# Dealing the work beside the selective scans by its products, with one pair's convolutions moved behind them and the first unit set up differently

## The chip, the cores and the metric

The kernel runs on one core of one Trainium2 chip. The metric is the device time of one execution in microseconds (us); before the change the median of three runs is 3226.97, from 3225.29 to 3227.04. A core has engines with queues of their own that work in order: PE (TensorE, matrix products; its weight loads are counted apart as PEld), DVE (VectorE), ACT (ScalarE), POOL (GpSimd) and SP, which issues DMAs. They wait for each other by semaphores.

## The reference

The program is a stack of layers on an input of 8 images of 128 channels and 16 x 16 points: an adder convolution, a "mamba" fusion layer, an attention with a mixture of experts, a performer and a spectral layer. All the diff's effect is in the second, cut here to what matters:

```python
xn = layer_norm(x); u, z = split(xn @ in_proj_w.T)          # 256 channels each
for s in ("f", "b", "s"):                                   # forward, backward, sliced order
    uc    = silu(causal_conv1d(u_s, conv_w, conv_b))        # 4 taps, per channel
    proj  = uc @ xw.T                                       # dt (8), B (16), C (16)
    delta = softplus(dt @ dw.T + db)
    for n in range(16):                                     # states
        h_n = scan over l:  h = exp(delta * A_n) * h + delta * uc * B_n
    y_s   = sum_n h_n * C_n + uc * D
out   = ((y_f + y_b + y_s) * silu(z)) @ out_proj_w.T
attn  = softmax(y_f^T y_b);  out_a = y_s attn               # per image, over channels
out_a = conv3x3(out_a, fuse1)
x     = x + conv3x3(concat(out_a, out), fuse2)
```

## The kernel before

The second layer treats the images by pairs: four pairs of 512 columns, channels on the partitions, so that a full matrix product has 512 columns. All is 32-bit; a product shows in the profile as two records. A pair has three units, one for each scan order (f, b, s): twelve units in all, in the list `units`. A unit runs 16 rounds, one for each state n.

A round (in `_scans`) is: POOL multiplies `du` with the broadcast row B (`dbu`, L695; tile `db` has three buffers); ACT copies the row C into PSUM (`pcs`, L697); DVE runs two scans of 512 columns, one for each half of the 256 channels (`st`, L702), each of which takes a decay tile `da` (three PSUM banks in turn, refilled by an exponential on ACT, L658, `decays`); DVE multiplies by C (`hc`, L712, three buffers); PE adds `hc` to `acc` by two products with the identity. Before round 0 of a unit PE sets `acc` up with two products, and after round 15 ACT copies it out as `y` (L726 to L730).

Beside each round two generators advance, one step each: `more`, which prepares the next unit (`prepare`), and `other`, which does what belongs to the pair (`beside`). A step is what lies between two `yield`s.

- `prepare`: for s first z and its Silu. Then for each half the depthwise convolution as products with diagonal matrices (`pconv`; four for f and b, seven instructions for s), with its bias added on ACT (`pre`, L603); Silu as three ACT passes and a product (`silu`, L560 to L563), on POOL but in the very first unit on DVE; the projection `pp`, whose result is copied (`proj`, L611) and stored to DRAM rows by SP (L614); for each half the product `pd` and the softplus (L629 to L639, the last two on POOL); and `du` (L641). At round 14 what is left of it runs at once, and SP issues the first loads of the next unit's B and C rows (`chunk`, L650).
- `beside(p)`: the layer norm and the projection u of the next pair (`norm(p + 1)`), and then the finish of the pair before, `F.pair(p - 1)`: `attention` for each of its two images, `gated` (three POOL passes, L835 to L839, and the product `pm`) and `convolutions` (two 3x3 convolutions of 18 products each, tile `conv`, one step for each two products; the second ends with the addition to X on DVE, L869). In pair 0 it is `F.load()`, two DMAs of the convolution weights. What is left of it after a pair's third unit runs at once.

Thus the convolutions of pairs 0, 1 and 2 lie beside the scans of pairs 1, 2 and 3, and pair 3's finish runs behind all scans, in `mamba_layer`, with a PSUM pool of its own (`l1fps`, four banks), with its two images in step and most of its elementwise work on DVE (`F.alone`).

Before the first unit there is nothing to hide behind: `norm(0)` and the first `prepare` run one after the other (the set-up). `norm(0)` multiplies X by a centring matrix (identity less 1/128), which POOL makes at the start of `_scans` (L504).

Instructions are not issued in the order of the program text: a planner takes them engine by engine, by what is ready in its own model of the machine, and by the place in the text where several are. So the steps give priorities, not a fixed order. The performer layer behind raises the first 16 steps of its first stream (pairs 0 and 1) to the place marked by `E.mark`, the start of pair 3's finish.

Memory is given out in pools. A pool opened over memory that older pools have left waits either for all users of the older pools (the default), or, with `reuse_waits="tile"`, each tile for the older tiles under it. The performer's and spectral pools already have the latter. In the kernel before, `l1fps` lies over the three `da` banks and the bank of tag `s` in the scans' PSUM pools; `ln_rstd` and its neighbours in `l1one` lie over the adder layer's input x.

Of the kernel before, what the change touches and what calls it, by code (L numbers as in the profile page):

```python
# [207 lines left out]
class Env:  # L208


    def __init__(self, ctx, tc, dram, cols):
        self.tc, self.nc, self.dram = tc, tc.nc, dram
        self.cols = cols
        nc = self.nc
        pool = ctx.enter_context(tc.tile_pool(name="shared", bufs=1))
        self.pool = pool
        self.cst = pool.tile([P, dram["cst"].shape[1]], F32, tag="cst", name="cst")
        self.vecs = pool.tile([P, dram["vecs"].shape[1]], F32, tag="vecs", name="vecs")
        self.rows = pool.tile([P, dram["rows"].shape[1]], F32, tag="rows", name="rows")
        self.mean = pool.tile([P, P], F32, tag="mean", name="mean")  # L220
        self.ones = pool.tile([P, P], F32, tag="ones", name="ones")
        self.eps = pool.tile([P, 1], F32, tag="eps", name="eps")
        self.sg = pool.tile([P, NK], F32, tag="sg", name="sg")
        nc.gpsimd.memset(self.mean, 1.0 / P)
        nc.gpsimd.memset(self.ones, 1.0)
        nc.gpsimd.memset(self.eps, 1e-5)
        self.X = pool.tile([P, NT], F32, tag="X", name="X")

        self.early = ExitStack()
        early = self.early.enter_context(tc.tile_pool(name="early", bufs=1))  # L230
        self.w = {
            k: (pool if k in ("tok", "enc", "dec") else early).tile(
                list(dram[k].shape), F32, tag="w_" + k, name="w_" + k
            )
            for k in ("in_proj", "xproj", "dtproj", "out_proj", "tok", "enc", "dec")
        }

        self.diag = early.tile([P, 3, 2, 5, P], F32, tag="diag", name="diag")
# [84 lines left out]
def adder_layer(E):  # L323
# [8 lines left out]
    with ExitStack() as ctx:  # L332
# [54 lines left out]
        for kw in range(3):  # L387
            t = p.tile([P, B, 18 * 16], F32, tag=f"sh{kw}", name=f"sh{kw}")
            nc.gpsimd.tensor_copy(t.rearrange("p b (h w) -> p b h w", w=16), pad[:, :, :, kw : kw + 16])
            shifted.append(t)  # L390
        diagonals(E)
# [66 lines left out]
NPAIRS = B // UB  # L458
CN = 2


def mamba_layer(E):


    tc = E.tc
    with ExitStack() as ctx:
        F = _Fuse(E, ctx)
        with ExitStack() as inner:
            _scans(E, inner, F)
        F.psum = ctx.enter_context(tc.tile_pool(name="l1fps", bufs=4, space=PSUM))  # L470
        F.alone = True
        E.mark = tc.cur_priority
        for _ in F.pair(NPAIRS - 1):
            pass
# [11 lines left out]
def _scans(E, ctx, F):  # L486
# [7 lines left out]
    one = ctx.enter_context(tc.tile_pool(name="l1one", bufs=1))  # L494
    two = ctx.enter_context(tc.tile_pool(name="l1two", bufs=2))
    scratch = ctx.enter_context(tc.tile_pool(name="l1dram", bufs=2, space=bass.MemoryType.DRAM))
    pda = ctx.enter_context(tc.tile_pool(name="l1pda", bufs=1, space=PSUM))
    ps = ctx.enter_context(tc.tile_pool(name="l1ps", bufs=1, space=PSUM))
# [4 lines left out]
    center = one.tile([P, P], F32, tag="center", name="center1")  # L503
    nc.gpsimd.tensor_sub(center, E.c("ident"), E.mean)  # L504
    three = ctx.enter_context(tc.tile_pool(name="l1three", bufs=3))
    xn, us = {}, {}

    def norm(p):

        first = p == 0  # L510
        src = E.X[:, blk(p)]
        pxc = ps.tile([P, UT], F32, tag="s" if first else "f", name="xc1")
        E.mm(pxc, center, src)
        xc = one.tile([P, UT], F32, tag="ln_xc", name="ln_xc")
        if first:
            nc.vector.tensor_copy(xc, pxc)
        else:
            nc.scalar.copy(xc, pxc)
        rstd = one.tile([P, UT], F32, tag="ln_rstd", name="ln_rstd")
        nc.scalar.activation(rstd, pxc, AF.Square)  # L520
        yield
        var = ps.tile([P, UT], F32, tag="f", name="var1")
        E.mm(var, E.mean, rstd)
        nc.scalar.activation(rstd, var, AF.Ln, bias=E.eps)

        nc.scalar.activation(var, rstd, AF.Exp, scale=-0.5)
        yield
        t = xn[p] = two.tile([P, UT], F32, tag="xn", name="xn1")
        nc.vector.tensor_mul(t, xc, var)
        nc.scalar.activation(t, t, AF.Identity, scale=E.v("ln_w"), bias=E.v("ln_b"))  # L530
        yield
        us[p] = two.tile([P, 2, UT], F32, tag="u", name="u1")
        for h in range(2):
            pu = ps.tile([P, UT], F32, tag="s" if first and h else "f", name="pu")
            E.mm(pu, E.w["in_proj"][:, h * P : (h + 1) * P], t)
            dst = us[p][:, h, :]
            if first and h:
                nc.vector.tensor_copy(dst, pu)
            else:
                nc.scalar.copy(dst, pu)  # L540
            yield
# [15 lines left out]
    def silu(dst, src, gen):  # L557

        t = one.tile([P, 2, UT], F32, tag="sig", name="sig")
        nc.scalar.activation(t, src, AF.Exp, scale=-1.0)  # L560
        nc.scalar.activation(t, t, AF.Ln, bias=E.ones[:, 0:1])
        nc.scalar.activation(t, t, AF.Exp, scale=-1.0)
        gen.tensor_mul(dst, src, t)  # L563
        return t

    def prepare(k, s, p, got, first=False):
        u = us[p].rearrange("p h (b l) -> p h b l", l=L)
        if s == "s":
# [6 lines left out]
            yield  # L575
            silu(z, z, nc.gpsimd)
            yield
        uc = two.tile([P, 2, UT], F32, tag="uc", name="uc")
        pre = one.tile([P, 2, UT], F32, tag="pre", name="pre")
        for h in range(2):  # L580
# [15 lines left out]
            for j, (m, out, src) in enumerate(taps):  # L596
                E.mm(out, E.diag[:, k, h, 3 - m, :], src, start=j == 0, stop=j == len(taps) - 1)
            dst = pre[:, h, :].rearrange("p (b l) -> p b l", l=L)
# [5 lines left out]
            yield  # L604
        room = silu(uc, pre, nc.vector if first else nc.gpsimd)
        yield
# [9 lines left out]
        yield  # L616
# [6 lines left out]
        for h in range(2):  # L623
# [7 lines left out]
            yield  # L631
# [4 lines left out]
            yield  # L636
# [3 lines left out]
            yield  # L640
        gen.tensor_mul(du, delta, uc)  # L641
        got.update(delta=delta, du=du)
        yield
# [9 lines left out]
    turns = [0, 0]  # L653

# [6 lines left out]
    def beside(p):  # L661
# [4 lines left out]
        else:  # L666
            yield from F.pair(p - 1)
# [7 lines left out]
    for i, (k, s, p) in enumerate(units):  # L675
# [8 lines left out]
        for n in range(NST):  # L684
# [30 lines left out]
            next(more, None)  # L715
            next(other, None)
# [18 lines left out]
class _Fuse:  # L735


    def __init__(self, E, ctx):
        self.E = E
        nc, tc = E.nc, E.tc  # L740
        one = ctx.enter_context(tc.tile_pool(name="l1fone", bufs=1, side="right"))
        self.two = ctx.enter_context(tc.tile_pool(name="l1ftwo", bufs=2, side="right"))
        self.four = ctx.enter_context(tc.tile_pool(name="l1ffour", bufs=4, side="right"))
# [23 lines left out]
    def pair(self, p):  # L767
        images = [self.attention(self.y[p], b) for b in range(UB)]
        if self.alone:
            while images:  # L770
                images = [g for g in images if next(g, None)]
        else:
# [3 lines left out]
        yield from self.convolutions(p)  # L776

    def attention(self, y, b):
# [4 lines left out]
        for k in range(2):  # L783
# [7 lines left out]
            yield True  # L791
# [13 lines left out]
        yield True  # L805
# [6 lines left out]
        yield True  # L812
# [6 lines left out]
        yield True  # L819
# [7 lines left out]
        yield True  # L827

    def gated(self, p):
# [6 lines left out]
        yield True  # L836
        gen.tensor_add(g, g, y[:, 2])
        yield True
        gen.tensor_mul(g, g, self.z[p])  # L839
        yield True  # L840
# [7 lines left out]
        yield True  # L848

    def convolutions(self, p):  # L850
        E, nc = self.E, self.E.nc
        for j in range(2):
            out = self.bank([P, UT], "conv")
            for n in range(18):
# [3 lines left out]
                if n % 2:  # L858
                    yield True
# [10 lines left out]
            yield True  # L870
# [193 lines left out]
def performer_layer(E, W):  # L1064
# [3 lines left out]
    with ExitStack() as ctx:  # L1068
# [19 lines left out]
        S.center = one.tile([P, P], F32, tag="center", name="center")  # L1088
        nc.vector.tensor_sub(S.center, S.c("ident"), S.mean)
# [529 lines left out]
```

## Time and profile before

| what | us | from |
|---|---|---|
| median of three runs | 3226.97 | times |
| the profiled execution | 3226.58 | times |
| its span | 3224.5 | page |
| adder layer, to the last addition to X | 0 to 988.5 | timeline |
| set-up to the first scan | 988.65 to 1032.50 | timeline |
| scans, 192 rounds | 1032.50 to 1799.36 | timeline |
| pair 3's finish | 1799.4 to 1854.6 | timeline |
| the layers behind | 1854.6 to 3224.5 | timeline |

| engine | busy us over the span | share |
|---|---|---|
| PE | 2994.3 | 93% |
| DVE | 2395.7 | 74% |
| ACT | 2208.3 | 68% |
| POOL | 733.2 | 23% |

A line of the timeline or of a group names the line of the code, the engine, the instruction, the output and its inputs, the shape and how many records; in brackets is how long the engine had been idle before and what ended that. Nearly all matrix products have the line of one helper, L271, and so are told apart by tiles. Shares over the whole span say little about this change: PE's 93% is an average over an adder layer and a performer that keep it full, and the scans, where DVE has the most to do. What a change in the scans is worth must be read there.

### The profile page before, as it was taken

How to read it: one execution, taken by the hardware profiler on the slowest of the kernel's cores; microseconds unless marked ns; L12 is line 12 of the kernel's file. 1: busy time of each engine (PE TensorE's matmuls, PEld its weight loads, DVE VectorE, ACT ScalarE, POOL GpSimd, SP SyncE). 2: the span in 40 equal slices, each digit the busy share in tenths (PEclk: the TensorE clock that was granted, in tenths of full speed). 3: DMA queues.
4: the chain of work that ended last, by engine and by line, in shares of the span. 5: the costliest groups of instructions: out<-in, count | busy, mean ns of one | idle time of the engine just before them, and what ended most of it. 6: DMA issues, size and time to landing. Idle time of an engine off the chain costs nothing.

```text
span 3224.5 us, 42745 instructions
## 1 busy us (share of the span) xinstructions
PE 2994.3 (93%) x16814; PEld 1335.5 (41%) x16814; DVE 2395.7 (74%) x3288; ACT 2208.3 (68%) x2639; POOL 733.2 (23%) x420
## 2 busy tenths in 40 slices
PE   6999999999997888888988789999999999999999
PEld 2333332333332333333343345555555555555444
DVE  6999999999995999788897466665665566564531
ACT  6999999999995877677675243666657766667111
POOL 3000000000002888677786100100000010010110
PEclk9999999999998999999999999999999999999999
DMA  1000000000001544333343100000000000000200
GB/s 38 1 1 5 1 1 4 1 1 5 1 1 59 178 146 136 124 126 126 120 143 115 47 27 14 1 15 1 15 14 1 15 14 1 14 1 3 86 27 13
DMA packets 39197, 132.53 MB, mean 41 GB/s; under 512 B 7490, under 2 KB 10572, under 8 KB 36564
## 3 DMA queue, kind: packets, MB, share of 16 engines
q1 hardware_dynamic: 38564, 129.07, 11.9%
q8 instruction: 132, 2.16, 0.3%
q10 hardware_dynamic: 432, 0.73, 0.1%
q14 instruction: 69, 0.57, 0.1%
HBM read 126.91 MB, written 1.84 MB: 40 GB/s over the span
## 4 chain that ended last, share of the span: by engine, by line
PE 69%; DVE 14%; ACT 6%; issue 5%; POOL 4%; DMA 1%; DVEq 0%; POOLq 0%; ACTq 0%; SPq 0%
PE o L271 29%; PE p L271 8%; DVE hc L712 4%; DVE st L702 4%; PE g L271 3%; PE pc L271 3%; PE acc L271 2%; PE pq L271 2%; PE xc L271 2%; PE pa L271 2%; PE conv L271 2%; PE pn L271 2%; PE pb L271 2%; PE var L271 1%; PE po L271 1%
## 5 line engine op out<-in xcount | busy, mean ns | idle before, releaser
L271 PE MATMUL o<-d,sel 128*32 128x512 f32 x8800 | 946.5, 592 | 3.2 <-DVE d L437 3.2
L439 ACT ACTIVATE d<-sh,w 128x2048 f32<-128x2048 f32 x460 | 886.3, 1996 | 64.2 <-PE o L271 54.8
L437 DVE TENSOR_SCALAR d<-sh,w 128x2048 f32<-128x2048 f32 x640 | 787.0, 1287 | 48.9 <-PE o L271 41.0
L271 PEld LDWEIGHTS o<-d,sel 128*32 128x32 f32 x8800 | 298.2, 110 | 650.7 <-issue 540.9
L695 POOL TENSOR_TENSOR dbu<-du,bs 128x1024 f32<-128x1024 f32 x191 | 449.2, 2365 | 171.8 <-DVE st L702 75.1
L702 DVE TENSOR_TENSOR_SCAN st<-da,dbu 128x512 f32<-128x512 f32 x384 | 448.4, 1206 | 30.5 <-POOL dbu L695 17.9
L271 PE MATMUL acc<-hc,cst 128*128 128x512 f32 x768 | 369.2, 609 | 56.6 <-DVE hc L712 56.3
L658 ACT ACTIVATE da<-delta,neg_a 128x510 f32<-128x510 f32 x384 | 260.0, 688 | 118.2 <-DVE st L702 112.8
L712 DVE TENSOR_TENSOR hc<-st,pcs 128x1024 f32<-128x1024 f32 x192 | 229.9, 1197 | 48.1 <-PE acc L271 38.8
L1278 POOL TENSOR_TENSOR rk<-rk,ro 128x512 f32<-128x512 f32 x32 | 40.8, 1274 | 911.6 <-DVE ro L1277 911.6
L271 PEld LDWEIGHTS acc<-hc,cst 128*128 128x128 f32 x768 | 140.6, 192 | 249.4 <-issue 139.0
L748 POOL MEMSET pad<- 128x1296 f32 x2 | 2.3, 1177 | 952.3 <-PE o L271 952.3
L1551 ACT COPY ug<-p 128x512 f32<-128x512 f32 x64 | 37.5, 586 | 176.3 <-PE p L271 176.3
L697 ACT COPY pcs<-cs 128x512 f32<-128x512 f32 x192 | 113.5, 591 | 57.9 <-DVE hc L712 55.6
L271 PE MATMUL p<-u,lw 128*128 128x512 f32 x256 | 132.7, 637 | 16.5 <-ACT ek L1323 14.7
L271 PE MATMUL conv<-pad,f 128*128 128x512 f32 x288 | 135.7, 601 | 8.6 <-ACT pad L845 4.4
L431 DVE SCALAR_TENSOR_TENSOR d<-sh,w,d 128x2048 f32<-128x2048 f32 x52 | 122.3, 2351 | 1.9
L271 PE MATMUL p<-T,H 128*128 128x512 f32 x256 | 114.4, 596 | 5.7 <-DVE ug L1553 4.7
L1374 ACT ACTIVATE qp<-px,keps 88x512 f32<-88x512 f32 x128 | 84.2, 678 | 50.9 <-PE px L1373 50.5
L271 PE MATMUL p<-g,lw 128*128 128x512 f32 x256 | 114.6, 595 | 0.8 <-ACT g L1216 0.8
L271 PE MATMUL g<-ug,me 128*128 128x512 f32 (+1 forms) x320 | 112.0, 509 | 2.0 <-DVE me L1539 2.0
L1323 ACT ACTIVATE ek<-ek 128x352 f32<-128x352 f32 x128 | 60.1, 493 | 62.8 <-DVE ek L1320 62.7
(317 smaller groups left out, 4166.9 us busy)
## 6 DMA issues: line engine op xcount, KB each, us to landing
bs<-rows SPq DMA_DIRECT2D x96, 512.0 KB, 3.8
cs<-rows SPq DMA_DIRECT2D x96, 512.0 KB, 4.7
lw<-in_layers SPq DMA_DIRECT2D x8, 1076.0 KB, 4.9
m<-in_Mphi SPq DMA_DIRECT2D x8, 1024.0 KB, 4.9
f<-in_fuse SPq DMA_DIRECT2D x2, 1152.0 KB, 7.7
T<-in_T SPq DMA_DIRECT2D x1, 2064.0 KB, 8.0
x<-in_x SPq DMA_DIRECT2D x4, 256.0 KB, 6.3
total<-sums SPq DMA_DIRECT2D x16, 64.0 KB, 2.0
```

The lines of the kernel that those rows point to most:

```text
L271: self.nc.tensor.matmul(out, lhsT=lhsT, rhs=rhs, start=start, stop=stop)
L431: nc.vector.scalar_tensor_tensor(held, tap(k), w[:, k, f : f + 1], held, ALU.max, ALU.add)
L437: nc.vector.tensor_scalar(d, tap(k), wk, None, ALU.max)
L439: nc.scalar.activation(d, tap(k), AF.Abs, scale=-1.0, bias=wk)
L658: nc.scalar.activation(das[turns[0] % 3][:, :, 1:], d[:, :, 1:], AF.Exp, scale=a)
L695: gen.tensor_tensor(db, got["du"], bc(got["bs", c][:, j, :], 1, 2), ALU.mult)
L697: nc.scalar.copy(pcs, got["cs", c][:, j, :])
L702: nc.vector.tensor_tensor_scan(st[:, h, :], da.rearrange("p b l -> p (b l)"), db[:, h, :], 0.0, ALU.mult, ALU.add)
L712: nc.vector.tensor_tensor(hc, st, bc(pcs[:, :], 1, 2), ALU.mult)
L1278: nc.gpsimd.tensor_add(r, r, o)
L1323: nc.scalar.activation(e, e, AF.Exp, scale=0.5)
L1374: nc.scalar.activation(qp[:, :, c * P : (c + 1) * P], px, AF.Identity, bias=S.keps[0:PAIR, :])
```

## The change

- **Dealing.** Every step now yields a cost, about the number of 512-column products that it holds (0.1 for a step without any). A round gets a budget of `SHARE` = 2.25; what `more` costs is taken off (one step a round, as before), and `other` advances as long as some budget is left; an overdraft carries over to the next round.
- **Finer steps.** A half's depthwise convolution is cut into two steps, a 3x3 convolution yields after each product. The softplus has one step less a half: the subtraction and addition on POOL follow its exponentials without a yield between.
- **The third pair's convolutions.** `F.pair` is split into `before` (attention and gate) and `convolutions`. In pair 3 the scans only take `before(2)`; pair 2's convolutions run behind the scans, four steps of them after each step of pair 3's attention and gate, and then pair 3's.
- **The first unit.** Silu's three passes and its product are done for each half as soon as the half is there. The centring matrix is made in the adder layer, in the shared pool, and the performer uses the same one. `norm(0)` works on the centred values in PSUM, without a copy, and writes its reciprocal root to SBUF.
- **Pools.** All pools of the layer get `reuse_waits="tile"`. The Silu's work tile of z and of uc are taken apart by name (same tag).

```diff
@@ adder_layer
+        nc.gpsimd.tensor_sub(E.center, E.c("ident"), E.mean)
         diagonals(E)
@@ mamba_layer
-        F.psum = ctx.enter_context(tc.tile_pool(name="l1fps", bufs=4, space=PSUM))
+        F.psum = ctx.enter_context(tc.tile_pool(name="l1fps", bufs=4, space=PSUM, reuse_waits="tile"))
         F.alone = True
         E.mark = tc.cur_priority
-        for _ in F.pair(NPAIRS - 1):
-            pass
+        last = NPAIRS - 1
+        convs = F.convolutions(last - 1)
+        for _ in F.before(last):
+            for _ in range(4):
+                next(convs, None)
+        for p in (convs, F.convolutions(last)):
+            for _ in p:
+                pass
@@ _scans, norm
-        E.mm(pxc, center, src)
-        xc = one.tile([P, UT], F32, tag="ln_xc", name="ln_xc")
-        if first:
-            nc.vector.tensor_copy(xc, pxc)
-        else:
+        E.mm(pxc, E.center, src)
+        xc = pxc
+        if not first:
+            xc = one.tile([P, UT], F32, tag="ln_xc", name="ln_xc")
             nc.scalar.copy(xc, pxc)
...
-        nc.scalar.activation(var, rstd, AF.Exp, scale=-0.5)
+        r = rstd if first else var
+        nc.scalar.activation(r, rstd, AF.Exp, scale=-0.5)
@@ _scans, prepare
             for j, (m, out, src) in enumerate(taps):
                 E.mm(out, E.diag[:, k, h, 3 - m, :], src, start=j == 0, stop=j == len(taps) - 1)
+                if j + 1 == len(taps) // 2:
+                    yield 2
...
-            yield
-        room = silu(uc, pre, nc.vector if first else nc.gpsimd)
-        yield
+            if h == 0:
+                room = one.tile([P, 2, UT], F32, tag="sig", name="sig")
+            if first:
+                silu(uc[:, h, :], pre[:, h, :], room[:, h, :], nc.vector)
+            yield 2
+        if not first:
+            silu(uc, pre, room, nc.gpsimd)
+            yield 0.1
...
             nc.vector.scalar_tensor_tensor(e, one_e, -1.0, e, ALU.add, ALU.subtract)
-            yield
             nc.scalar.activation(r, one_e, AF.Ln)
             gen.tensor_sub(r, r, e)
             gen.tensor_add(d, d, r)
-            yield
+            yield 0.1
@@ _scans, beside and the rounds
-            yield from F.pair(p - 1)
+            yield from F.before(p - 1)
+            if p + 1 < NPAIRS:
+                yield from F.convolutions(p - 1)
...
-            next(more, None)
-            next(other, None)
+            budget = min(budget, 0) + SHARE - next(more, 0)
+            while budget > 0:
+                cost = next(other, None)
+                if cost is None:
+                    break
+                budget -= cost
@@ _Fuse.convolutions
-                if n % 2:
-                    yield True
+                yield 1
```

The costs given elsewhere: 1 for each step of `norm` but its scaling (0.1); 2 for z's products, 2 for a half of a depthwise half, 2 for `pp`, 1 for each `pd`; in attention 0.6 for each set of four transposes, 2 for the scores, 2 for the output, 0.1 for the scaling; in the gate 0.1 for each of the three passes and 2 for `pm`; 0.1 behind each 3x3 convolution.

## The prediction

> **What bounds the kernel now.** I read the table of stages first, then DVE's waits inside the scans, then PE's timeline where they are longest, then the two ends: the first unit's set-up and the stretch behind the scans. All times are of the profiled execution (3226.58 us, span 3224.5), 0.4 us below the median of the runs, 3226.97; my sum is made against 3226.6.
>
> By stages (columns: stretch, its length, busy us of PE, weight loads, DVE, ACT, POOL, granted clock, DMA share, GB/s). The first four are the four pairs of images in the scans, cut where the last `hc` of a pair's 48 rounds ends; the fifth is what stands behind them.
>
> ```profile
> 1037.10:1203.90 166.80, 133.50 (x292) 50.92 (x292) 163.89 (x150) 130.97 (x210) 141.66 (x67) 0.98 0.48 161
> 1203.90:1402.30 198.40, 170.91 (x414) 73.52 (x414) 172.17 (x158) 138.18 (x229) 152.11 (x71) 0.98 0.39 131
> 1402.30:1607.00 204.70, 179.33 (x432) 76.64 (x432) 172.69 (x159) 142.36 (x236) 150.67 (x71) 0.96 0.38 124
> 1607.00:1799.40 192.40, 163.56 (x398) 72.05 (x398) 170.01 (x156) 126.33 (x209) 135.81 (x71) 0.96 0.37 127
> 1799.40:1854.60 55.20, 48.55 (x138) 25.44 (x138) 11.68 (x25) 5.92 (x18) 0.11 (x1) 0.94 0.04 17
> ```
>
> Pair 0 has DVE busy for 163.9 of 166.8 us: it is bound by the scans, and its undisturbed rounds repeat every 3.36 us. Pairs 1 and 2 carry the finish of the pair before (attention, gate, two 3x3 convolutions) and last 198.4 and 204.7 with DVE busy only 172: 58.2 us are lost. Pair 3 loses 22.4. DVE's waits in pairs 1 and 2 (1204 to 1607; total us, times, longest):
>
> ```profile
> DVE hc L712 <- PE acc L271: 27.3, 8, 6.0
> DVE st L702 <- POOL dbu L695: 10.0, 4, 3.8
> DVE hc L712 <- ACT da L658: 4.5, 1, 4.5
> DVE st L702 <- ACT da L658: 4.2, 3, 2.4
> ```
>
> In pair 3 the first two are 11.5 and 6.5. `hc` has three buffers, so it waits for `acc` only when PE is three rounds of backlog behind. How that comes about, in pair 3's second unit:
>
> ```profile
> 1695.85 3.71 PE L271 MATMUL pconv<-u,diag 128*128 128x512 f32 x14 [1.46 <-ACT pre L603]
> ...
> 1699.39 1.88 PE L271 MATMUL conv<-pad,f 128*128 128x512 f32 x4
> ...
> 1703.10 1.22 DVE L712 TENSOR_TENSOR hc<-st,pcs 128x1024 f32<-128x1024 f32 x1 [4.94 <-PE acc L271]
> ```
>
> One round got a whole half of the depthwise convolution and convolution products on top of its own two; DVE stood for 4.94 us. Behind the scans PE is nearly full:
>
> ```profile
> 1796.93 1.98 PE L271 MATMUL acc<-hc,cst 128*128 128x512 f32 x4 [1.38 <-DVE hc L712]
> 1799.41 1.98 PE L271 MATMUL acc<-hc,cst 128*128 128x512 f32 x4 [0.50 <-DVE hc L712]
> 1802.56 1.97 PE L787 MATMUL pt<-cst,y 128*128 128x128 f32 x16 [1.16 <-ACT y L730]
> ...
> 1811.59 1.09 PE L816 MATMUL pt<-cst,at 128*128 128x128 f32 x4 [2.61 <-DVE at L809]
> 1813.81 0.45 PE L816 MATMUL pt<-cst,at 128*128 128x128 f32 x1 [1.13 <-DVE at L809]
> ...
> 1821.52 15.62 PE L271 MATMUL conv<-pad,f 128*128 128x512 f32 x36
> ```
>
> A 512-column product is two records; 36 records in 15.6 us make **0.86 us a product** back to back. That unit is used below.
>
> **Part 1, ahead of the scans.** Now `center` (POOL, 0.45) starts only when the last X addition is out, and the first product waits for it:
>
> ```profile
> 988.65 0.45 POOL L504 TENSOR_TENSOR center<-cst,mean 128x128 f32<-128x128 f32 x1 [3.24 <-DVE X L452]
> 989.16 2.07 PE L271 MATMUL xc<-X,center 128*128 128x512 f32 x2 [6.19 <-POOL center L504]
> ```
>
> With the matrix made early and tile-wise reuse, the product needs X's first block alone (985.68 + 0.71 = 986.4) and is done by 988.5. Its square on ACT, at 991.99 before, needs `ln_rstd`'s bytes, which lie in the old x that the last addition reads until 988.55: about 988.65, so 3.3 us earlier. That takes the product 2.1 (hidden behind the additions), the copy `ln_xc` 0.7 and center 0.5 off the path. POOL's subtraction moves into the first layer, where POOL is idle: nothing. If the wait is by block rather than by tile it is 5; if something else in the old bytes is late, 1. Silu by halves: behind the last `pre`, three ACT passes of 1024 columns (1.06 + 1.15 + 1.06) and one DVE product (1.23) become 512-column ones; rows of that size take 0.60, 0.69, 0.60 and 0.69: 4.5 against 2.6, 1.9 saved; the first half's pass lies under the second half's products (pre ends 1008.4 and 1011.8). Together **-5.2**, bounds -2.5 and -7.
>
> At one place here the clock matters. The four xproj records `pp` took 3.32 us after PE had idled 5.39; in the scans the same four take 1.91, and the granted clock was 0.82 from 1002 to 1032. [...] I take nothing for it.
>
> **Part 2, the dealing, pairs 1 and 2.** Work now comes by cost: each round gets 2.25 products beside its own two. A pair's cost by the new yields: preparing f and b 12.4 each, s 14.5; norm 4.1; attention and gate 14.1; convolutions 36.2: 93.7 in 48 rounds, so 41.6 rounds at 4.25 products, 3.66 us on PE (above DVE's 3.36), and 6.4 at 3.36: 152.3 + 21.5, plus six first products of `acc`, 5.2: **179** against DVE's busy 172. No round now gets more than 5 products. So the 27.3 us on `acc` go, and the pacing replaces them. What dealing does not touch: waits for POOL 10.0, for `da` 8.7, for `pcs` 4.0, 22.7 in all; a DVE wait in a PE-paced round lets PE catch up, so I count half, 11.4. PE's own waits for POOL's `uc` before `pp` (12.3 us in 8 places from 1204 to 1800) stay, with three convolution products between in place of two; about 4 in these pairs. 2 x 179 + 15.4 = 373 against 403.1: **-30**. Bounds: -48 (DVE busy 344.9 plus the POOL waits alone) and +10 (the old waits stay and the pacing is paid too). Pair 0 has 1.5 us of POOL wait and bursts to lose: **-2**, 0 to -3.
>
> What the moved steps issue: F.load's two DMAs on SP go from about round 5 to round 6 of the first unit; their first user is at 1298. The `rows` store on SP comes two rounds later (7 us); its loads are issued at round 14, more than 5 rounds behind. Delta's last step keeps its round (the tenth for f and b). In the gate three POOL passes of 2.36 now fall in one round, since each costs 0.1; POOL's lead is `db`'s three buffers, two rounds or 6.7 us, against 7.1: small, and inside the bounds.
>
> **Part 3, pair 3 without convolutions.** DVE busy 170.0, less the X addition 0.7, plus the waits for POOL and small ones (6.5 + 2.0), plus a quarter of the `acc` waits (those at attention in the first unit stay, 3): 181 against 192.4: **-12**; bounds -18 and -5.
>
> **Part 4, behind the scans.** 36 products come here: 36 x 0.86 = 31.0. They can fill PE's idle 0.50 + 1.16 + 2.61 + 1.13 = 5.4: **+25.8**. Upper bound +31. `l1fps` lies over the banks of the three `da` and of `s`; tile-wise, `s`'s bank is free all through the last unit and `da2`'s before the last round, where PE idles 1.38 a round. If the scheduler pulls attention and convolutions there, and the next layer's first half starts beneath the convolutions, it is +10. I take +25.8, since three banks come free only at the end. The 0.93 between the last two convolutions and the last X addition stay; the SBUF tiles and performer's work keep their sizes.
>
> Sum: -5.2 - 30 - 2 - 12 + 25.8 = -23.4, **3203 us**.
>
> **Rivals.** (A) Slower: PE has no slack left at 4.25 products a round, and its in-order queue still waits for POOL's `uc`, itself behind gate passes; each such wait is now paid in full. For: PE idled 12.3 us before `pp`, POOL is busy 152 of 198. Pairs 1 and 2 then keep their length (0), pair 3 gains 5, the ends -2.5 and +31: 3250. It decides as soon as pairs 1 and 2 together gain less than 6.6 (25.8 - 5.2 - 2 - 12). Against: PE in these pairs is busy 171 and 179 of about 200, so 50 us of slots exist. (B) The convolutions only change place: pair 3 gains 12, pairs 1 and 2 about 15, the tail costs 31, with -5.2 and -2 elsewhere: -3, 3223; within what can be told. For: 31 us of work into a stretch that is 88% PE. (C) Better than summed: pairs 1 and 2 near DVE's bound (-42), pair 3 -16, tail +18 because bank `s` and the performer's head start fill it: -47, 3179. For: the free bank and the 1.38 us gaps. (D) The change doesn't do what it says: the order on each engine is the planner's, by what is ready, so that the convolutions are pulled back among pair 3's last rounds; the tail is then +10 and the last unit 5 longer, 3192: inside the forecast's range.
>
> **How the numbers follow.** Forecast with D 0.51, C 0.22, B 0.10, A 0.17. The predicted time is the forecast's. 0.2% (6.5 us) is about what can be told from no change, and B alone lies within it. Faster 0.73, same 0.10, slower 0.17. Range: down to C, up past 3226 until little of A is inside: 3177 to 3232.
>
> **What would show it.** Right: DVE's waits for `acc` in pairs 1 and 2 under 10 us, rounds of 3.6 to 3.7 with few above 6, the pairs 183 to 190 long; pair 3 near 180; 72 more `conv` records behind the scans and that stretch some 80 us; the first scan 5 us earlier. Wrong: pairs still near 200 with waits now for POOL or `da`, or the stretch behind the scans over 90.

## The result, and the profile after

The changed kernel takes **3300.43 us** (median of four runs, 3297.98 to 3301.82), beside 3226.91 for the kernel before on the same chip (four runs, 3225.29 to 3227.04). The ratio is 1.0228, with a 95% interval from 1.0210 to 1.0246: slower, where 3203 and "faster" had been predicted, and above the range's end of 3232. The profiled execution's span is 3297.7 us against 3224.5, so 73.2 us have to be found.

The stages of the kernel after, cut in the same way as those of the kernel before (columns: stretch, its length, busy us of PE, weight loads, DVE, ACT, POOL, granted clock, DMA share, GB/s):

```profile
1032.40:1217.90 185.50, 141.43 (x297) 53.41 (x296) 163.73 (x151) 131.88 (x211) 141.82 (x67) 0.94 0.43 145
1217.90:1431.90 214.00, 180.13 (x414) 76.83 (x415) 173.03 (x158) 137.48 (x228) 150.11 (x71) 0.91 0.36 119
1431.90:1654.00 222.10, 185.01 (x432) 78.63 (x432) 174.46 (x159) 141.40 (x236) 150.66 (x71) 0.93 0.34 115
1654.00:1847.70 193.70, 142.06 (x326) 60.03 (x326) 167.42 (x154) 125.17 (x207) 137.90 (x71) 0.90 0.39 128
1847.70:1926.10 78.40, 77.30 (x212) 37.78 (x212) 12.55 (x25) 6.75 (x20) 0.11 (x1) 1.00 0.03 12
```

DVE has about the same work as before in every pair (163.7, 173.0, 174.5 and 167.4 us against 163.9, 172.2, 172.7 and 170.0), and each pair is longer, pair 0 too, which has no finish of another pair beside it. Pair 3 lost its 72 `conv` records (398 to 326) and is no shorter. The granted clock is lower in all four pairs: 0.94, 0.91, 0.93 and 0.90 against 0.98, 0.98, 0.96 and 0.96. Where the 73.2 us lie, the tail being the time from the last scan round to the last addition to X, and the forecast of -30 for pairs 1 and 2 halved between them (the terms are rounded, so the last digit of a row's sum may differ):

| us | to the first `hc` | pair 0 | pair 1 | pair 2 | pair 3 | tail | layers behind | sum |
|---|---|---|---|---|---|---|---|---|
| forecast | -5.2 | -2 | -15 | -15 | -12 | +25.8 | 0 | -23.4 |
| measured | -4.6 | +18.7 | +15.6 | +17.4 | +1.3 | +23.2 | +1.7 | +73.2 |

The two ends came as forecast. The 12 units' scans did not. DVE's waits inside all scans of the kernel before, and then of the kernel after (total us, times, longest):

```profile
DVE hc L712 <- PE acc L271: 38.8, 12, 6.0
DVE st L702 <- POOL dbu L695: 17.9, 7, 4.9
```

```profile
DVE hc L728 <- PE acc L272: 45.8, 18, 7.0
DVE st L718 <- POOL dbu L711: 45.2, 13, 8.7
DVE hc L728 <- ACT pcs L713: 16.7, 13, 2.8
```

The waits for `acc`, which the dealing was to remove from pairs 1 and 2, are still there (in these two pairs alone 39.7 us, for 27.3 before). The waits for `dbu` grew from 17.9 to 45.2 us. And PE itself, in the kernel before and in the kernel after, from the same view:

```profile
PE pp L271 <- POOL uc L563: 15.2, 11, 3.0
```

```profile
PE pp L272 <- POOL uc L571: 43.0, 11, 5.6
```

PE stands at `pp`, the projection of the next unit, for 43.0 us in 11 places; the prediction had priced that at about 4 in pairs 1 and 2.

**Where the `dbu` waits sit.** I measured each of the 192 rounds from the end of one `hc` to the end of the next. Of the eleven first rounds (round 0 of every unit but the first) I add up what is over 3.36 us: 2.8 us in the kernel before and **50.0 us** in the kernel after, where the longest last 13.9, 12.3 and 18.2 us. The start of the last unit in the kernel after, on POOL (timeline; columns: start, length, instruction, in brackets the idle time before it and what ended that):

```profile
1778.23 1.27 POOL L651 TENSOR_TENSOR sig<-sig,pre 128x512 f32<-128x512 f32 x1 [9.20 <-ACT sig L650]
...
1786.03 1.27 POOL L651 TENSOR_TENSOR sig<-sig,pre 128x512 f32<-128x512 f32 x1 [5.18 <-ACT sig L650]
...
1788.72 2.34 POOL L654 TENSOR_TENSOR du<-delta,uc 128x1024 f32<-128x1024 f32 x1
1791.14 9.25 POOL L711 TENSOR_TENSOR dbu<-du,bs 128x1024 f32<-128x1024 f32 x4
```

and what DVE's timeline has for it:

```profile
1784.49 0.69 DVE L649 SCALAR_TENSOR_TENSOR pre<-one_e,pre 128x512 f32<-128x512 f32 x1 [4.55 <-ACT one_e L648]
1793.51 3.52 DVE L718 TENSOR_TENSOR_SCAN st<-da,dbu 128x512 f32<-128x512 f32 x3 [8.33 <-POOL dbu L711]
```

The old unit's scans are over; the new unit's softplus is still going through PE, ACT and POOL; `du` is out at 1791.06 and the first scan follows `dbu`, after 8.33 us in which DVE had nothing. In the kernel before the same `du` was out at 1735.54 and DVE stood for 4.86 there, its longest wait for `dbu`. In the kernel after the preparation comes too late. The means over all 11 preparations, and in the last column the sum of the first rounds:

| kernel | `pp` starts after the unit's first scan | `pp` to the end of `du` | `du`'s end against the unit's last scan | first rounds over 3.36, sum |
|---|---|---|---|---|
| before | 32.7 | 27.2 | 2.2 early | 2.8 |
| after | 40.4 | 26.5 | 3.0 late | 50.0 |

`dbu` takes 2.36 us behind `du`, and a scan cannot start before it. So the kernel before had on the mean no margin left to give, and the change took 5.2 us.

### The profile page after: what moved, and what is told of

Its sections match the earlier page's. It is cut to its first block, busy times and chain, and to the rows that moved or that the text cites. A ratio compares the mean times of both kernels' runs of the same rounds, so it can differ in the third digit from the quotient of the medians.

```text
span 3297.7 us, 42745 instructions
## 1 busy us (share of the span) xinstructions
PE 3025.5 (92%) x16814; PEld 1344.4 (41%) x16814; DVE 2398.2 (73%) x3287; ACT 2207.2 (67%) x2642; POOL 733.8 (22%) x420
## 4 chain that ended last, share of the span: by engine, by line
PE 69%; DVE 13%; issue 6%; POOL 6%; ACT 5%; DMA 1%; DVEq 0%; POOLq 0%; ACTq 0%
PE o L272 29%; PE p L272 8%; DVE hc L728 4%; PE g L272 3%; DVE st L718 3%; PE pc L272 3%; PE conv L272 3%; PE acc L272 2%; PE pq L272 2%; POOL dbu L711 2%; PE pa L272 2%; PE xc L272 2%; PE pn L272 2%; PE pb L272 2%; PE var L272 1%
## 5 line engine op out<-in xcount | busy, mean ns | idle before, releaser
L718 DVE TENSOR_TENSOR_SCAN st<-da,dbu 128x512 f32<-128x512 f32 x384 | 449.2, 1207 | 61.4 <-POOL dbu L711 45.2
L272 PE MATMUL acc<-hc,cst 128*128 128x512 f32 x768 | 383.4, 627 | 76.8 <-DVE hc L728 76.4
L272 PE MATMUL pconv<-u,diag 128*128 128x512 f32 (+7 forms) x240 | 97.2, 533 | 12.6 <-ACT pre L612 7.6
```

Source lines behind the costliest of these rows:

```text
L272: self.nc.tensor.matmul(out, lhsT=lhsT, rhs=rhs, start=start, stop=stop)
L718: nc.vector.tensor_tensor_scan(st[:, h, :], da.rearrange("p b l -> p (b l)"), db[:, h, :], 0.0, ALU.mult, ALU.add)
```

## The experiments

The **lateness theory (L)** says: the depthwise convolution's new yield in the middle of a half makes `pp` two rounds later, the chain behind it is as long as before in time, and each unit's first scan waits for `du`. The **rivals**: PE's in-order queue stands at `pp` for POOL's `uc` (43.0 us, for 15.2 before), with the convolution products behind it, and that is what lengthens the pairs, whether `du` is late or not; the dealing itself, with its 2.25 products a round, leaves PE no slack; or one of the other parts (moved convolutions, set-up, pools, the softplus without its yields) costs. The ratios are to the kernel before in the same comparison, with 95% intervals.

### Each part alone

**e1: the changed kernel without the yield in the half.**

```diff
-                if j + 1 == len(taps) // 2:
-                    yield 2
...
-            yield 2
+            yield 4
```

> The changed kernel with one part undone: a half of the depthwise convolution is again one step (cost 4 in place of 2 + 2), so preparing a unit takes two rounds less. Theory L (late preparation: the two added steps bring du two rounds later, and the first scan of a unit stands for it): the waits of st for dbu fall from 45 to below 22, most rounds 0 of units are under 5 us, and the time falls by 35 to 55, to 3245-3265. Theory P (PE has no slack at 4.25 products a round, and its queue waits for uc at pp): the split only spreads products, so undoing it gives bursts back: 3295-3315. Theory Y (the softplus without its yields holds POOL): within 10 us of 3300.

Measured: 3241.90 us (3233.75 to 3244.25), ratio 1.0042 [1.0027, 1.0057]. Without that yield, two steps less in a preparation, 58 of the 73 us come back, a little more than the 35 to 55 expected. (The profiled execution is the shortest of its four, so the stages read from it are some 8 us below the median run, and what is read from them for e1 alone is known no closer.) `pp` starts at 34.3 after the unit's first scan, `du` is 4.2 us early, the first rounds are down to 7.8 us. From `pp` to the end of `du` the chain takes 24.3 us here, so with the lead given back the softplus without its yields is some 3 us shorter than before. DVE's waits and the stages of pairs 1 and 3 in e1:

```profile
DVE hc L726 <- PE acc L272: 27.8, 14, 8.0
DVE st L716 <- POOL dbu L709: 9.0, 6, 2.6
```

```profile
1206.30:1397.70 191.40, 168.33 (x419) 72.63 (x419) 171.53 (x158) 139.67 (x231) 152.12 (x71) 1.00 0.40 138
...
1599.10:1781.50 182.40, 137.04 (x328) 57.15 (x328) 169.59 (x153) 124.91 (x207) 135.60 (x71) 0.96 0.40 131
```

Without the yield pair 1 is 7.0 shorter than in the kernel before and pair 3 is 9.8 shorter; against them stand the tail, 78.4 for 55.2, and pair 0, 176.0 for 166.8.

**e2: the kernel before with only that yield.**

```diff
                 E.mm(out, E.diag[:, k, h, 3 - m, :], src, start=j == 0, stop=j == len(taps) - 1)
+                if j + 1 == len(taps) // 2:
+                    yield
```

> The kernel before with the split of the depthwise halves alone, one step a round as it was. Theory L: preparation two rounds later, first rounds of units stand: 3250-3275. Theory P: bursts in pairs 1 to 3 get smaller, nothing else: 3215-3227. Theory Y: same as before, 3220-3230.

Measured: 3268.32 (3267.50 to 3269.28), ratio 1.0129 [1.0114, 1.0144]: +41. The two additional steps of a preparation put `du` 4.3 us behind the last scan, 6.5 later than before, close to two rounds of 3.36. DVE's waits in e2:

```profile
DVE st L704 <- POOL dbu L697: 51.6, 10, 8.7
DVE hc L714 <- PE acc L271: 34.3, 17, 5.6
```

The `dbu` waits are those of the changed kernel, and more; the `acc` waits are about those of the kernel before. The first rounds are 59.3 us over; some of it is won back in other rounds, since the scans as a whole are 41.8 longer.

**e5: the kernel before with only pair 2's convolutions moved behind the scans** (two of its steps, four products, after each step of pair 3's attention and gate).

```diff
-        for _ in F.pair(NPAIRS - 1):
-            pass
+        last = NPAIRS - 1
+        convs = F.convolutions(last - 1)
+        for _ in F.before(last):
+            for _ in range(2):
+                next(convs, None)
+        for p in (convs, F.convolutions(last)):
+            for _ in p:
+                pass
...
-            yield from F.pair(p - 1)
+            yield from F.before(p - 1)
+            if p + 1 < NPAIRS:
+                yield from F.convolutions(p - 1)
```

> The kernel before with pair 2's convolutions behind the scans alone (two steps of two products after each step of pair 3's attention and gate). All theories: pair 3's scans shorter by 12 to 17 (it loses 22 to waits, 11.5 of them on acc), the stretch behind longer by 22 to 26 (the changed kernel has 77.4 against 55.2): 3232-3242. If the planner fills the last rounds or the next layer starts earlier: 3215-3225.

Measured: 3237.18, ratio 1.0040 [1.0026, 1.0054]: +9.9. Its pair 3 and what stands behind the scans, by stages:

```profile
1607.00:1786.00 179.00, 138.40 (x326) 58.54 (x326) 168.04 (x154) 124.22 (x207) 135.76 (x71) 0.94 0.41 136
1786.00:1864.50 78.50, 76.42 (x210) 37.40 (x210) 12.65 (x26) 6.76 (x20) 0.11 (x1) 1.00 0.03 12
```

Pair 3 is 13.3 shorter (192.4 to 179.0) and the tail 23.3 longer (55.2 to 78.6): the move costs 10 by itself in the kernel before. (From e1 to e8 below, which take it back, it is 13.6.)

**e4: the kernel before with only the early centring matrix, the layer norm from PSUM, the first unit's Silu by halves, and the pools' waits by tile.**

```diff
+        nc.gpsimd.tensor_sub(E.center, E.c("ident"), E.mean)
         diagonals(E)
...
-        E.mm(pxc, center, src)
+        E.mm(pxc, E.center, src)
...
+            if first:
+                silu(uc[:, h, :], pre[:, h, :], room[:, h, :], nc.vector)
```

> The kernel before with the set-up part alone: centring matrix early, first Silu by halves, the norm's PSUM path, tile-wise reuse in all pools; no dealing, no split, nothing moved. The changed kernel's first scan stands 4.6 us earlier (1027.87 against 1032.50): 3220-3224 by theories L and P. If tile-wise reuse has changed the planner's order for the worse, and is the loss: 3250 or more.

Measured: 3228.25, ratio 1.0007 [0.9997, 1.0016]; 3220 to 3224 had been expected. The first scan starts at 1024.4, 8.1 us earlier than in the kernel before, and nothing of it is left at the end: pair 0 takes 173.8 in place of 166.8 and pair 1 202.8 in place of 198.4. In pair 0 the trace of e4 shows where: DVE waits 7.5 us there, against 1.5 us (once, for `dbu`) in the kernel before:

```profile
DVE hc L715 <- ACT pcs L700: 3.4, 4, 1.6
DVE st L705 <- POOL dbu L698: 2.6, 1, 2.6
DVE st L705 <- ACT da L661: 1.5, 1, 1.5
```

Two of its preparations have a `pp` of 3.57 and 3.63 us in place of 1.91; ACT stands 3.3 us each time for the result, and the copy of C that the next `hc` needs is queued behind. Why `pp` is slow in just these two stays open.

**e8: the dealing without the yield in the half and without the move** (e1 with pair 2's convolutions beside pair 3's scans again; so it holds the set-up and the pools of e4 and the shorter softplus as well).

```diff
-        convs = F.convolutions(last - 1)
+        convs = iter(())
...
             yield from F.before(p - 1)
-            if p + 1 < NPAIRS:
-                yield from F.convolutions(p - 1)
+            yield from F.convolutions(p - 1)
```

> The changed kernel without the split and with pair 2's convolutions again beside pair 3's scans: dealing by cost, the set-up part, the softplus without its yield and the tile-wise pools stay. From the run without the split (3241.9), undoing the move should give back what the move alone cost (+9.9): 3226-3236. If dealing needs the room that the move makes in pair 3: 3242 or more.

Measured: 3228.27, ratio 1.0006 [0.9997, 1.0015]: no difference, in place of the 30 us forecast. By pairs it is +8.9, -5.4, -2.1 and +8.1 against the kernel before: what pairs 1 and 2 gain, pairs 0 and 3 lose. Waits in e8, DVE's and PE's in all scans, and then DVE's in pairs 1 and 2 alone, where the kernel before has 27.3:

```profile
DVE hc L725 <- PE acc L272: 46.7, 20, 8.0
DVE st L715 <- POOL dbu L708: 9.1, 6, 2.6
...
PE pp L272 <- POOL uc L571: 28.1, 11, 4.0
```

```profile
DVE hc L725 <- PE acc L272: 28.9, 14, 8.0
```

The dealing did not take these waits away, and PE's timeline ahead of the longest of them, in pair 2, shows how that one comes about:

```profile
1489.34 7.14 PE L272 MATMUL conv<-pad,f 128*128 128x512 f32 x16 [1.49 <-ACT pad L863]
1496.31 1.02 PE L272 MATMUL acc<-hc,cst 128*128 128x512 f32 x2
...
1497.37 1.22 DVE L725 TENSOR_TENSOR hc<-st,pcs 128x1024 f32<-128x1024 f32 x1 [8.01 <-PE acc L272]
```

Eight convolution products stand in one run between two rounds' `acc` products, although a round is dealt 2.25. In pairs 1 and 2 the longest such run between two rounds' products has 14 records of all kinds in the kernel before, 30 in e8, and 24 in the changed kernel, 18 of them `conv`. The steps are dealt evenly in the program, but the planner does not put them into PE's queue that way; how it comes to this order was not tried.

### Lateness by itself, with no work moved

**e6 and e7: the kernel before with one, or two, empty steps in `prepare`.** In e7 it is `range(2)`. No instruction is added or cut in two.

```diff
             yield
+        for _ in range(1):
+            yield
         uc = two.tile([P, 2, UT], F32, tag="uc", name="uc")
```

> The kernel before with one empty step more in preparing a unit, ahead of its depthwise convolution, so that all behind it comes one round later; no split, nothing else. Theory L (what the split costs is the delay itself): a loss, but a small one, since there were some rounds of margin: 3230-3245. Rival S (the split costs by where it cuts the products or by the planner's order): same as before, 3222-3230.

> The same with two empty steps, as many as the split adds. Theory L: the loss of the split alone, 3268, within 12 us (3256-3280), and again rounds 0 in which st stands for dbu by 5 to 12 us. Rival S: 3222-3232.

Measured: e6 3254.56, ratio 1.0086 [1.0069, 1.0103], +28, more than the 3230 to 3245 expected; e7 3278.41, ratio 1.0158 [1.0143, 1.0173], +52. `du` ends 0.1 us before the end of the unit's last scan in e6 and 4.3 us behind it in e7, the very value of e2, and the first rounds are 26.9 and 59.3 us over. DVE's wait for `dbu` in e7:

```profile
DVE st L704 <- POOL dbu L697: 51.6, 10, 8.7
```

The line is e2's to the last digit, though e7 cuts no convolution: the delay makes the wait, not the finer steps. The scans are longer by 26.4 us in e6 and 43.7 in e7, beside 41.8 in e2; of the 10 us by which e7 is slower than e2 as a whole, 5.4 lie in the layers behind and 2.3 ahead of the scans. That one step already costs 28 shows that the kernel before stood on the edge.

**e10: the kernel before with two steps of `more` in rounds 0 and 1**, so that a preparation begins two steps ahead.

```diff
             next(more, None)
+            if n < 2:
+                next(more, None)
             next(other, None)
```

> The kernel before with preparation two rounds earlier: two steps of it in rounds 0 and 1. Theory L with a margin that was already enough: 3218-3230, since before's rounds 0 lose only 3 us in all. If before's waits for POOL (17.9) and for pp's uc (15.2) also come from lateness: 3200-3215. If bursts decide (two steps, up to 14 products' records in a round): 3235 or more.

Measured: 3229.19, ratio 1.0007 [0.9997, 1.0017]. `du` is now 8.2 us early on the mean in place of 2.2, and nothing is gained: pair 0 is 3.7 longer, pair 1 3.2 shorter. Lateness costs; two steps of earliness do not pay here.

**e14: the changed kernel, its yield kept, with the same two steps ahead.**

```diff
             budget = min(budget, 0) + SHARE - next(more, 0)
+            if n < 2:
+                budget -= next(more, 0)
```

> The changed kernel whole with the split kept, but two steps of preparation in rounds 0 and 1, so that the two added steps are made up. Theory L: as the run without the split, 3242, within 10 us. If the split costs by itself (finer products, other order): 3265 or more.

Measured: 3243.59, ratio 1.0052 [1.0037, 1.0068]: 57 of the 73 us are back, as in e1, with the half still cut in two. (Here the profiled execution is the longest of its four, 6 us above the median.) `du` is 3.4 us early. DVE's waits in e14:

```profile
DVE st L718 <- POOL dbu L711: 15.9, 6, 6.9
DVE hc L728 <- PE acc L272: 34.5, 19, 5.1
```

So the cut itself costs nothing that can be told but its delay.

### PE's stand at `pp`

**e11: the dealing (e8) with the last Silu product on DVE**, so that `pp` does not wait for POOL.

```diff
         if not first:
-            silu(uc, pre, room, nc.gpsimd)
+            silu(uc, pre, room, nc.vector)
```

> Dealing without split and without the move (3228), with the product uc of Silu on DVE in place of POOL. If PE's stand at pp for uc costs time of its own: PE's wait for uc falls from 28 to under 10, DVE's wait for acc from 47 to under 30; DVE gets 11 x 1.2 = 13 us more to do; 3205-3222. If the stands only show lateness or backlog elsewhere: DVE's added 13 us are paid, 3235-3245.

Measured: 3232.03, ratio 1.0025 [1.0015, 1.0036], between what the two theories expected. Waits in e11, PE's and DVE's:

```profile
PE pp L272 <- DVE uc L571: 11.5, 9, 3.1
...
DVE hc L725 <- PE acc L272: 36.0, 14, 6.9
```

Against e8 PE stands 16.6 us less and DVE waits 10.7 us less for `acc`, but DVE takes over 11 products of some 1.2 us, 13 us. Where nothing is late, avoiding the stand costs about what it brings.

**e12: the dealing (e8) with an empty step between the Silu and `pp`.**

```diff
             yield 0.1
+            yield 0.1
         proj = one.tile([NPROJ, UT], F32, tag="proj", name="proj")
```

> The same kernel (3228) with one empty step between Silu's product and pp; preparing has 10 steps then, one less than before the change. If pp's place in the order follows the step: PE's wait for uc falls by half, 3212-3224. If it follows the planner's own time of readiness: the wait stays and a round of delay is paid, which with fewer steps than before should be little: 3228-3245.

Measured: 3230.78, ratio 1.0016 [1.0007, 1.0025]. PE's stand at `pp` goes from 28.1 only to this:

```profile
PE pp L272 <- POOL uc L571: 25.1, 11, 4.3
```

A round of distance in the program did not bring `pp` behind its operand: where PE's queue gets it seems to be the planner's model of when `uc` is ready, not the step. That reading is argued from this one run.

**e13: the changed kernel with the last Silu product on DVE.**

> The changed kernel whole, with the product uc on DVE. Theory L alone: the delay stays, uc comes some 2 us earlier a unit, DVE pays 13: 3285-3305. If the stand of PE at pp is a second cause: PE's wait falls from 43 to under 15 and the clock granted in the scans rises from 0.92 to 0.96: 3255-3280.

Its edit is that of e11. Measured: 3271.48, ratio 1.0141 [1.0127, 1.0155], 29 us faster than the changed kernel. Waits in e13:

```profile
DVE st L718 <- POOL dbu L711: 44.9, 12, 8.3
DVE hc L728 <- PE acc L272: 11.9, 7, 5.0
...
PE pp L272 <- DVE uc L571: 18.9, 10, 5.3
```

The lateness is untouched (44.9 against 45.2), `du` is still 3.1 us late; what went is 33.9 us of waits for `acc`. The edit also takes 11 products off POOL, but the waits for POOL did not move, so the gain is put down to PE's stand: in the late kernel, and only there, it is a second cause worth some 29 us. The granted clock over the scans rose only from 0.92 to 0.93 where 0.96 was expected, with 18.9 us of stands at `pp` in place of 43.0: the low clock does not come from these stands alone.

No version tried beats the kernel before: e8, e4 and e10 equal it, e12 and e11 are 0.16 and 0.25% slower, and all others by more.

## Why the prediction was wrong, point by point

**The lateness: the step that failed.** The prediction wrote of the moved steps "Delta's last step keeps its round (the tenth for f and b)", and of the `rows` store and its loads that there were "more than 5 rounds" between them. So it put the two yields ahead of `pp` at nothing. The count is right: two yields came in ahead of `pp` and two went out of the softplus behind it. But steps are not time. From `pp` to the end of `du` the chain of PE, ACT, DVE and POOL took 27.2 us before and 26.5 after, about eight rounds, with two steps less in it (in e1, with its lead given back, 24.3). Nearly all that was put ahead of `pp` thus went through to the end: `pp` 7.7 us later, `du` 5.2 us later against the unit's end, where the margin was 2.2. The number was in the trace of before: `du` of the last unit ended 3.5 us behind the scans of the unit ahead of it, but the table of stages does not show it. What showed it: e1 and e14 take the lateness away in two different ways and get back 58 and 57 us; e2 and e7 add it to the kernel before and pay 41 and 52. Of the parts in the sum, this term stood at nothing.

**The dealing, -30 in pairs 1 and 2: the second step that failed.** The prediction took it that each round gets 2.25 products beside its own two, that "No round now gets more than 5 products", and that "the 27.3 us on `acc` go". PE's queue does not hold to that: in e8 runs of up to 30 records stand between two rounds' `acc` products, for 14 before, and 28.9 us of the waits in pairs 1 and 2 remain. (Even in the program, by the diff's own costs, one round of each of these pairs gets 5.7.) With lateness out of the way pairs 1 and 2 take 392.7 us together in e1 (a short run), 395.6 in e8 and 401.3 in e14 (a long one), against 403.1: a gain of 2 to 10. PE's stand at `pp` is the other source: 28.1 us in all scans of e8, where the prediction took about 4 for the two pairs. e11 shows the link: 16.6 us less at `pp` make 10.7 us less at `acc`. And what the dealing gains in pairs 1 and 2 is lost elsewhere. Pair 0, forecast at -2, takes 175.7 in e8 for 166.8; in e4, without the dealing, it is already 7.0 longer, so most of that seems to belong to the set-up's part. Pair 3 with its convolutions takes 200.4 for 192.4, and not so in e4 (192.2).

**Pair 3, -12: right as a mechanism.** Alone it is -13.3 (e5), in e1 -9.8. (The sum behind it, 181 against 192.4, makes -11.4.) In the changed kernel it is +1.3, since the last unit's first round alone lasts 18.2 us, 14.8 over, and PE's stands come on top.

**The tail, +25.8: right.** Measured +23.2 in the changed kernel and +23.3 in e5. PE's timeline behind the scans of the kernel after shows that the gaps are filled as reckoned:

```profile
1849.55 1.04 PE L808 MATMUL pt<-cst,y 128*128 128x128 f32 x8
1850.43 3.60 PE L272 MATMUL conv<-pad,f 128*128 128x512 f32 x8
```

PE is busy 77.3 of 78.4 us there, so there was no more to fill. Rival D, that the planner pulls the convolutions back among the scans, did not happen: all 144 `conv` records lie behind the last `hc`.

**The set-up, -5.2: right where it was measured, worth nothing at the end.** The first scan is 4.6 us earlier (1032.5 to 1027.9), although the adder layer's last addition ended 2.4 later (990.9 for 988.5), which was not pursued. The first product no longer waits for the centring matrix, and the square on ACT follows the end of the additions:

```profile
988.84 2.08 PE L272 MATMUL xc<-X,center 128*128 128x512 f32 x2 [3.51 <-DVE X L454]
...
991.15 0.58 ACT L528 ACTIVATE ln_rstd<-xc 128x512 f32<-128x512 f32 x1
```

Reckoned from the end of these additions the set-up is 7.0 shorter. The square comes 3.2 us earlier, for 3.3 in the sum, and from the last `pre` to `uc` it is 1.8, for 1.9. The rest lies behind, above all in `pp`, for which the prediction took nothing: all four records took 3.32 us after 5.39 of idle, and now the last two take 1.05 after 1.30. But e4, which has only this part, starts its scans 8.1 earlier and ends level.

**Rival A** stood nearest, at 3250, for PE's queue waiting on `uc`. Its mechanism is real and is worth 29 us in the late kernel (e13), but it was not what decided: e1 keeps 29.7 us of it and is 58 us faster. The rival with the right place, the lead of a preparation over its unit, was not on the list.

**The clock.** The prediction took nothing for a slower clock in the scans. One `pp` of the kernel before, then one of the kernel after, both from the timeline, the stretch around the latter as a window (its columns are those of the stages), and a `pp` of e4:

```profile
1706.67 1.91 PE L271 MATMUL pp<-uc,w_xproj 128*40 128x512 f32 x4 [0.26 <-POOL uc L563]
```

```profile
1330.86 3.64 PE L272 MATMUL pp<-uc,w_xproj 128*40 128x512 f32 x4 [4.17 <-POOL uc L571]
1336.61 1.22 DVE L728 TENSOR_TENSOR hc<-st,pcs 128x1024 f32<-128x1024 f32 x1 [7.05 <-PE acc L272]
```

```profile
1330.00:1337.00 7.00, 6.14 (x8) 1.41 (x8) 0.40 (x1) 0.86 (x2) 3.10 (x2) 0.54 0.12 31
```

```profile
1114.91 3.57 PE L272 MATMUL pp<-uc,w_xproj 128*40 128x512 f32 x4 [1.46 <-POOL uc L562]
```

After 4.17 us of idle the same four records take 3.64 in place of 1.91, the granted clock is 0.54 in those 7 us, and DVE stands 7.05 us for the `acc` products queued behind. But the gap just ahead does not decide alone in these traces: in e4 the four records took 3.57 us after only 1.46 of idle and in the kernel after one group took 3.32 after 1.44, while in the kernel before two took 1.91 after 1.79 and 1.81, and three took 3.22 to 3.63 after 2.80 to 3.05. The stand at 1330.86 is paid twice, with 4.17 us in waiting and 1.73 more in the products. How many of the 73 us are the clock's share was not separated.

**What is shown and what is open.** Shown: lateness from the yield costs 57 to 58 us in the changed kernel and 41 to 52 in the kernel before; the moved convolutions 10; the dealing, the set-up and the shorter softplus together nothing that can be told; PE's stand 29 within the lateness (it overlaps with the 58 and is not added to it). 58 + 10 and a remainder of about 5 make the 73. Open: why PE's stand grows from 28 to 43 us when the preparation is late; why the planner runs the convolution products together; why two `pp` of pair 0 are slow after the early start; and the softplus without its two yields, which was not tried alone.

## What to carry to other kernels

Before a step is put into a software pipeline, measure in the trace how long the chain behind it takes in time and how much margin its last product has before its user (here 2.2 us on the mean, against 3.36 a step); a count of steps does not say how long a chain through four engines takes. Work that is dealt evenly in the program need not run evenly: where a planner orders the instructions, look in the engine's own timeline for the longest run between two rounds (here 30 records after the dealing, for 14 before). And where an engine stands for an operand, evenly dealt work queues behind the stand as well (in e11, 16.6 us less of PE's stand at `pp` made 10.7 us less of DVE's waits for `acc`). Work moved from a stretch where it is half hidden to one where the engine is nearly full loses by the difference (here 31 us of products put 23 on the tail and took 13 off the pair), and both sides could be priced beforehand from rows of the trace.

## What the runs showed of the hardware that was not expected

The same four matrix product records took nearly twice as long behind some 4 us of idle. In the traces of the kernel before and the kernel after, the groups of four `pp` records that ran unbroken inside the scans took 1.91 us behind at most 0.65 us of idle, 3.49 to 3.64 behind 3.82 us or more, and anything from 1.91 to 3.63 behind 1.44 to 3.10 us. Records of `pp` (minimum, median, maximum in ns), first the kernel before, then the kernel after, then e13:

```profile
L271 PE MATMUL pp<-uc,w_xproj x48: 592/608/1076, 1016.5 to 1708.0; 128*40 128x512 f32 x48
```

```profile
L272 PE MATMUL pp<-uc,w_xproj x48: 592/1061/1076, 1010.7 to 1769.4; 128*40 128x512 f32 x48
```

```profile
L272 PE MATMUL pp<-uc,w_xproj x48: 592/593/1076, 1011.3 to 1739.9; 128*40 128x512 f32 x48
```

With 43.0 us of stands ahead of `pp` the median record took 1061 ns, with 15.2 us 608, and with 18.9 us and the Silu product on DVE 593. PE stands there 10 or 11 times in each of the three; only in the kernel after, where the stands add up to the most, did the median record take nearly twice the shortest, 592 ns.
